# A fixed order of slots for layer 0's dense sums and for layer 1's support stage

## The chip, the cores and the metric

The kernel runs on one core of one Trainium2 chip. The time is the device time of one execution in microseconds (us), the median of several runs. A core has TensorE (PE in the profile, with its weight loads as a row of their own, PEld), VectorE (DVE), ScalarE (ACT), GpSimd (POOL) and SyncE (SP), which here only issues DMAs. Each engine takes its instructions in the order in which they stand in its queue; an instruction that waits holds up all that stand behind it.

## What is computed

A four-layer graph network on 4096 nodes with 256 features and a dense 4096 x 4096 matrix of zeros and ones. Only the first two layers matter here:

```python
# layer 0: attention with 8 heads; entries off the graph have logit 0, not minus infinity
node_feats = (x @ W.T + b).reshape(4096, 8, 32)
logits = leaky_relu(logit_parent[:, None] + logit_child[None, :], 0.2)
logits = where(adj != 0, logits, 0.0)
out = einsum('ijh,jhc->ihc', softmax(logits, axis=1), node_feats)
x = layernorm(x + out)
# layer 1
support = x @ weight
out = (diagonal(adj) + adj) @ support + bias
x = layernorm(x + out)
```

Layer 2 (attention with a top-p cut, two diffusion steps) and layer 3 (mean of neighbours, a product, relu) follow.

## The kernel before, in words

Rows are handled in 32 blocks of 128 (`NB = 32`, `P = 128`). Instructions outside `manual_schedule` regions are put in order for each engine by a scheduler that simulates the program: an instruction may be moved ahead of others that stand before it in the source, as soon as the simulation finds its inputs and its buffers ready. Inside a `manual_schedule` region the named engines keep the order of the source. Buffers are given out from pools: a name with `bufs=2` has two buffers in turn, and the third tile of the name waits until the first is read for the last time. Before the change there are two such regions, both in layer 2.

**Layer 0, dense sums (`sums0`, L412 to L565).** A first part computes the node features and the factors of the softmax. Then comes the loop over pairs of blocks, L530 to L565. It reads the adjacency matrix once, in 128 groups of 512 KB: for each pair `b` eight groups `g` of four block columns. A group is loaded into `a` by two DMAs on SP's queue (L538), cast by VectorE to `ar` (L540), multiplied by ACT into bytes `nb` (L543, twice), stored as bytes to the DRAM tensor `nad` from POOL's queue (L544), and used by TensorE as the stationary operand of 32 matmuls against `src`, the node features in a high and a low part (L550). `a`, `ar` and `nb` have two buffers each. The sums of a pair, `pz`, stay in PSUM (four buffers[...]) until VectorE closes the pair (L559 to L564) and the result `zd` is stored (L565).

In the same loop `factored(b)` prepares what the later attention multiplies: for each block VectorE builds `vf` (L515 to L517), and in three rounds ACT copies it to bfloat16, `gb` (L521, L523, L525), and VectorE subtracts the copy (L522, L524), so that three bfloat16 parts hold one float32. Two DMAs on POOL's queue then store `gb` to the DRAM tensor `gmd` (L527). `vf` and `gb` have two buffers. In the source two blocks are factored ahead of each pair's groups; nothing in their inputs depends on the pair.

`early_mask` (L248 to L260) prepares a part of the first mask of the attention in four of the later pairs: a load of bytes from `nad` (L255) and, before the first part, one of `gmd` (L251), both on SP's queue, and three VectorE instructions in each of these pairs (two L257, one L260).

After the loop the kernel reads a flag (L366) and, since the factors fit, skips the general path. The attention of layer 0 (L328 and around) follows, from 610 to 1322 us. Its accumulator `acc` [...]has two buffers. The layernorms of finished rows run on POOL between heads; those of the last eight blocks, the list `later`, are left to layer 1.

**Layer 1 (`layer1`, L766 to L811).** Its support stage takes four blocks at a time (`g`): TensorE transposes the rows of X (L108), ACT copies the result to one of two tiles `xT` (L109), TensorE multiplies it by `w1` (L781; each is two matmuls in the profile[...]) into `ps_sup`, and `split` takes that to XD in a high part by ACT (L126) and a low part by VectorE (L127). `ps_sup` has two buffers. `attention_weights` (L752 to L764) runs ahead of it and uses `ps_sup` too. The layernorms of `later` stand in groups 1 to 4, all on VectorE but for the two small POOL instructions of each (L88, L89). After the stage a row for the diagonal is made (L786).

The product (L793 to L811) then multiplies the adjacency with XD: four pieces per block are cast back from bytes (L204 on ACT, L206 on VectorE; eight buffers), written to DRAM as float32 for layer 2 by `keep` (L154 to L168, on SP's queue, with the diagonal piece added on POOL, L164), and used in 32 matmuls (L802) per block. The bytes come by DMAs on ACT's queue (L189). The scheduler mixes the first of this work into the support stage.

Of the kernel before, what the change touches and what calls it, by code (L numbers as in the profile page):

```python
# [23 lines left out]
P = 128  # L24
# [31 lines left out]
class Net:  # L56
# [136 lines left out]
    def adj_pieces(self, pool, nas, b, G=8):  # L193

        nc = self.nc
        at = b * P % self.IT
        if at == 0:
            nas[:] = self.bytes_of(pool, b)
        pieces = []
        for g in range(self.NB // G):  # L200
            a = pool.tile([P, G, P], F32R, name="adj_piece", bufs=2 * (self.NB // G))
            edges = nas[g][:, :, at:at + P].bitcast(FP8)
            if g % 2:
                nc.scalar.mul(a, edges, 2.0 ** 5)  # L204
            else:
                nc.vector.tensor_scalar_mul(a, edges, 2.0 ** 5)  # L206
            pieces.append(a)
        return pieces
# [6 lines left out]
    def layer0(self):  # L215
# [7 lines left out]
        with ExitStack() as ctx:  # L223
# [24 lines left out]
            def early_mask(work, part):  # L248

                if part == 0:  # L250
                    nc.sync.dma_start(gm0, gmd[0, :, 0:8, 0])  # L251
                two = slice(2 * part, 2 * part + 2)
                na0, sg0 = (work.tile([P, 2, H, C1], F32, name=name).rearrange("p s h c -> p (s h c)")[:, :512]
                            .bitcast(dt).rearrange("p (k i) -> p k i", k=2) for name, dt in (("nf", U8), ("v", FP8)))
                nc.sync.dma_start(na0, nad[0, :, two, :])  # L255
                for k in range(2):
                    nc.vector.tensor_scalar(sg0[:, k, :], first, nlc[:, 2 * part + k, 0:1], 2.0 ** -5,  # L257
                                            op0=ALU.is_ge, op1=ALU.mult, saturate=False)
                bits = [t.rearrange("p k i -> p (k i)").bitcast(U32) for t in (gt0[:, two, :], sg0, na0)]
                nc.vector.tensor_tensor(*bits, ALU.bitwise_and)  # L260

# [100 lines left out]
            self.later = later  # L362

# [48 lines left out]
    def sums0(self, both, nlc, fac, lpd, nad, zd, gmd, then, early_mask):  # L412
# [6 lines left out]
        with ExitStack() as ctx:  # L419
# [91 lines left out]
            def factored(b):  # L511

                v = work.tile([P, H, 2, C1], F32, name="vf")
                part = lambda i, k: src[:, b, i, k].rearrange("p (h c) -> p h c", h=H).bitcast(F32)
                nc.vector.tensor_add(v[:, :, 1, :], part(0, 0), part(0, 1))  # L515
                nc.vector.tensor_add(v[:, :, 0, :], part(1, 0), part(1, 1))
                nc.vector.tensor_mul(v[:, :, 0, :], v[:, :, 0, :], elc[:, b].unsqueeze(2).to_broadcast([P, H, C1]))  # L517

                gb = work.tile([P, H, 3, 2 * C1], BF16, name="gb")
                v = v.rearrange("p h s c -> p h (s c)")  # L520
                nc.scalar.copy(gb[:, :, 0, :], v)  # L521
                nc.vector.tensor_sub(v, v, gb[:, :, 0, :])  # L522
                nc.scalar.copy(gb[:, :, 1, :], v)  # L523
                nc.vector.tensor_sub(v, v, gb[:, :, 1, :])  # L524
                nc.scalar.copy(gb[:, :, 2, :], v)  # L525
                for half in range(2):
                    nc.gpsimd.dma_start(gmd[half, :, b], gb[:, half * H // 2:(half + 1) * H // 2].rearrange("p h s c -> p h (s c)"))  # L527

            G = 4
            for b in range(0, NB, 2):  # L530
                it, i = divmod(b * P, IT)
                pz = [psz.tile([P, 2, 512], F32, name="pz") for _ in range(2)]
                for q in range(2):
                    factored(b + q)
                for g in range(NB // G):
                    a = work.tile([P, 2, G, P], F32, name="a")
                    for q in range(2):
                        nc.sync.dma_start(a[:, q], self.adjt[b + q, :, g * G:(g + 1) * G, :])  # L538
                    ar = work.tile([P, 2, G, P], F32R, name="ar")
                    nc.vector.tensor_copy(ar, a)  # L540
# [3 lines left out]
                    nc.gpsimd.dma_start(nad[it, :, g * G:(g + 1) * G, i:i + 2 * P], nb.rearrange("p g q i -> p g (q i)"))  # L544
                    for q in range(2):
                        for k in range(G):
                            jc = g * G + k
                            for s in range(2):
                                for t in range(2):
                                    nc.tensor.matmul(pz[q][:, t, :W], ar[:, q, k, :], src[:, jc, t, s],  # L550
                                                     start=(jc == 0 and s == 0), stop=(jc == NB - 1 and s == 1))
                if NB - 12 <= b < NB - 4:
                    early_mask(work, (b - NB + 12) // 2)
                for q in range(2):
                    zt = work.tile([P, 2, H, C1], F32, name="zt")
                    by_head = [t.rearrange("p (h c) -> p h c", h=H) for t in
                               (pz[q][:, 0, :W], pz[q][:, 1, :W], total)]
                    of_row = lambda i: fac[:, i, b + q].unsqueeze(2).to_broadcast([P, H, C1])
                    nc.vector.tensor_mul(zt[:, 0], by_head[0], of_row(2))  # L559
                    nc.vector.tensor_sub(zt[:, 1], by_head[2], by_head[1])  # L560
                    nc.vector.tensor_scalar(self.deg[:, b + q:b + q + 1], zt[:, 1, 0, C:C1], -1.0, float(N),
                                            op0=ALU.mult, op1=ALU.add)
                    nc.vector.tensor_mul(zt[:, 1], zt[:, 1], of_row(3))
                    nc.vector.tensor_add(zt[:, 0], zt[:, 0], zt[:, 1])  # L564
                    (nc.sync if b == NB - 2 else nc.scalar).dma_start(zd[b + q], zt[:, 0])  # L565
# [186 lines left out]
    def attention_weights(self, psum):  # L752
# [3 lines left out]
        for c in range(2):  # L756
            pt = psum.tile([P, 512], F32, name="ps_sup")
            nc.tensor.transpose(pt[:A, :P], aw1[:, c, :], self.ident)
            nc.scalar.copy(w1[:, c, :], pt[:A, :P])
        for c in range(2):  # L760
            pt = psum.tile([P, 512], F32, name="ps_sup")
# [4 lines left out]
    def layer1(self):  # L766
        nc, tc, NB, D, X = self.nc, self.tc, self.NB, self.D, self.X
        with self.ctx1 as ctx:
# [4 lines left out]
            self.attention_weights(psum)  # L773
            for g in range(NB // 4):
                xT = self.transposed(psum, work, X[:, 4 * g:4 * g + 4, :], "xT", out=self.xT1[g % 2])
                if 1 <= g <= 4:
                    self.layernorm(work, self.later[g - 1], self.later[g - 1])
                for q in range(4):
                    ps = psum.tile([P, 512], F32, name="ps_sup")
                    for c in range(2):  # L780
                        nc.tensor.matmul(ps[:, :D], xT[:, c, q * P:(q + 1) * P], w1[:, c, :],  # L781
                                         start=(c == 0), stop=(c == 1))
                    self.split(XD[:, 4 * g + q], ps[:, :D])
            pd = psum.tile([P, 512], F32, name="ps_sup")
# [7 lines left out]
            nas = []  # L792
            ahead = self.adj_pieces(work, nas, 0)  # L793
# [1192 lines left out]
```

## Time and profile before

| what | us |
|---|---|
| runs before, median of 3 (lowest to highest) | 3985.94 (3985.65 to 3993.06) |
| the profiled execution | 3996.39 |
| its span, first to last instruction | 3994.6 |
| setup of layer 0, to the first L550 | 0 to 72.7 |
| dense sums, L550 | 72.7 to 605.1 |
| attention of layer 0, L328 | 610.5 to 1322.1 |
| support stage, to the last L786 | 1322.1 to 1395.65 |
| last L802 of the product | 1623.4 |
| layers 2 and 3 | to 3994.6 |

Times within the run are microseconds from the start of the span. A group of the profile is one line of code on one engine: after `|` come its busy time, the mean nanoseconds of one, and after the next `|` the engine's idle time just before such instructions, with what ended it (`<-`). A row of the window view gives a stretch, its length, the busy time of each engine with the number of instructions in brackets, then the TensorE clock that was granted (1.00 is full), the mean busy share of the 16 DMA engines, and GB/s.

### The profile page before, as it was taken

The numbers are of one execution on the slowest core, as the hardware profiler recorded it, in microseconds if no ns is written. First come the engines' busy times: TensorE is split into PE (matmuls) and PEld (weight loads), VectorE is DVE, ScalarE is ACT, GpSimd is POOL, SyncE is SP. The second block draws the span as 40 slices with busy tenths as digits, with TensorE's granted clock in tenths as the row PEclk, the third lists the DMA queues.
The fourth block names the chain that finished last, engine by engine and source line by source line (L and its number), as shares of the span: only waits on it lengthen the run. The fifth ranks groups of instructions, "written<-read, shape, count | busy, mean of one in ns | idle before, by whom it ended". The sixth has DMA issues, their size and how long they took to land. (4 is left out here: it accounts for less than half of the span.)

```text
span 3994.6 us, 68784 instructions
## 1 busy us (share of the span) xinstructions
PE 3901.5 (98%) x25081; PEld 3375.7 (85%) x25081; DVE 2997.9 (75%) x6645; ACT 2747.6 (69%) x5121; POOL 1160.1 (29%) x1394
## 2 busy tenths in 40 slices
PE   8899998999999899999999999999999999999899
PEld 7899998999999788668888888875888888888687
DVE  7642228999999544567878787847999999999364
ACT  5533227999999422468888888835988888888232
POOL 1321111111344022311111111114556555555311
PEclk9999999999999999999999999999999999999999
DMA  4765557335222498533232323373333333335641
GB/s 127 230 207 174 179 169 220 96 98 145 70 77 71 153 354 331 164 120 102 93 102 93 103 92 103 100 240 107 101 120 100 107 113 111 103 107 183 203 164 48
DMA packets 317563, 557.36 MB, mean 140 GB/s; under 512 B 72806, under 2 KB 139894, under 8 KB 313110
## 3 DMA queue, kind: packets, MB, share of 16 engines
q1 hardware_dynamic: 242528, 396.99, 31.2%
q0 software_dynamic: 32224, 98.75, 7.7%
q10 hardware_dynamic: 42454, 57.04, 4.3%
q8 instruction: 203, 3.33, 0.3%
q14 instruction: 154, 1.26, 0.1%
HBM read 386.71 MB, written 165.94 MB: 138 GB/s over the span
## 5 line engine op out<-in xcount | busy, mean ns | idle before, releaser
L1359 PE MATMUL ps_a<-X,aT 128*128 128x256 f32 x4096 | 968.9, 379 | 1.3 <-ACT h L1503 1.1
L1359 PEld LDWEIGHTS ps_a<-X,aT 128*128 128x128 f32 x4096 | 773.2, 190 | 127.0 <-issue 3.5
L328 PE MATMUL acc<-gm,gt 128*128 128x198 bf16 x8192 | 702.7, 248 | 14.1 <-DMA gm<-gmd 5.6
L328 PEld LDWEIGHTS <-gt 128*128 128x128 fp8e4 x8192 | 700.7, 97 | 16.2 <-issue 11.2
L273 ACT ACTIVATE sg<-lpb,nlc 128x1024 fp8e4<-128x1024 f32 x632 | 664.4, 1138 | 48.4 <-DVE gt L275 33.7
L550 PE MATMUL pz<-src,ar 128*128 128x264 f32 x4096 | 512.8, 288 | 20.1 <-DVE ar L540 18.1
L550 PEld LDWEIGHTS pz<-src,ar 128*128 128x128 f32 x4096 | 509.6, 191 | 23.2 <-DVE ar L540 21.4
L180 PE MATMUL ps_r<-XD,adj_piece 128*128 128x512 f32 x1888 | 528.4, 414 | 0.0
L1086 ACT ACTIVATE ja<-e,nc 128x2048 uint8<-128x2048 f32 x240 | 481.3, 2006 | 2.0
L1352 ACT COPY aT<-ps_tp 128x512 f32<-128x512 f32 x512 | 296.6, 579 | 214.4 <-PE ps_tp L1350 212.0
L180 PEld LDWEIGHTS ps_r<-XD,adj_piece 128*128 128x128 f32 x1888 | 332.9, 189 | 68.8 <-issue 12.9
L1151 DVE MAX8 cand<-v 128x8 f32<-128x256 f32 x1024 | 347.3, 414 | 4.4
L1201 DVE SCALAR_TENSOR_TENSOR e<-e,edge 128x512 f32<-128x512 f32 x512 | 346.6, 749 | 2.1
L543 ACT ACTIVATE nb<-ar 128x512 uint8<-128x512 f32 x256 | 147.8, 624 | 268.2 <-DVE ar L540 268.0
L1350 PE MATMUL ps_tp<-ident,e 128*128 128x128 f32 x2048 | 308.1, 273 | 1.9 <-DVE e L1201 1.9
L1147 DVE SCALAR_TENSOR_TENSOR v<-e,hi 128x2048 f32<-128x2048 f32 x128 | 303.1, 2368 | 2.3
L1350 PEld LDWEIGHTS ps_tp<-ident,e 128*128 128x128 f32 x2048 | 256.8, 142 | 53.6 <-DVE e L1201 3.0
L267 DVE TENSOR_SCALAR sg<-lpb,nlc 128x1024 fp8e4<-128x1024 f32 x384 | 286.1, 781 | 6.6 <-SPq L366 4.4
L995 ACT ACTIVATE e<-ps_logit 128x1024 f32<-128x1024 f32 x256 | 260.2, 1027 | 27.1 <-PE ps_logit L993 26.7
L993 PE MATMUL ps_logit<-kT,q 128*128 128x512 f32 x1024 | 273.5, 409 | 1.8 <-ACT e L995 1.4
L540 DVE CAST ar<-a 128x1024 fp32r<-128x1024 f32 x128 | 89.1, 696 | 247.2 <-PE pz L550 244.3
L802 PE MATMUL ps_adj<-XD,adj_piece 128*128 128x512 f32 x1024 | 244.8, 398 | 1.2 <-POOL ln_var L88 1.2
(401 smaller groups left out, 5614.4 us busy)
## 6 DMA issues: line engine op xcount, KB each, us to landing
adj_piece<-adjs SPq DMA_DIRECT2D x552, 256.0 KB, 2.8
a<-in_adjt_dram SPq DMA_DIRECT2D x256, 256.0 KB, 2.9
adjs<-adj_piece SPq DMA_DIRECT2D x96, 512.0 KB, 3.4
na<-nad SPq DMA_DIRECT2D x64, 512.0 KB, 4.3
lpb<-lpd POOLq DMA_DIRECT2D x32, 512.0 KB, 4.2
nad<-nb POOLq DMA_DIRECT2D x128, 128.0 KB, 2.7
na<-nad ACTq DMA_DIRECT2D x16, 1024.0 KB, 5.7
gmd<-gb POOLq DMA_DIRECT2D x64, 198.0 KB, 3.7
```

Source lines behind the costliest of these rows:

```text
L180: nc.tensor.matmul(ps, a[:, k, :], rhs(jc).rearrange("p s d -> p (s d)"), start=(jc == 0), stop=(jc == self.NB - 1))
L267: nc.vector.tensor_scalar(sg[:, k, :], lpb, nlc[:, 4 * g + k, h:h + 1], 2.0 ** -5, op0=ALU.is_ge, op1=ALU.mult, saturate=False)
L273: nc.scalar.activation(sg[:, k, :], lpb, AF.Sign, scale=-1.0, bias=nlc[:, 4 * g + k, h:h + 1], saturate=False)
L328: nc.tensor.matmul(acc[:, q, :6 * C1], gt[:, k, q * P:(q + 1) * P], gm0[:, jc, :] if head0 else gm[:, jc, hh, :], start=(jc == 0 and q % 2 ...
L550: nc.tensor.matmul(pz[q][:, t, :W], ar[:, q, k, :], src[:, jc, t, s], start=(jc == 0 and s == 0), stop=(jc == NB - 1 and s == 1))
L1086: nc.scalar.activation(ja, e[:, s * HALF:(s + 1) * HALF], f, bias=nc1, accum_out=fs[:, i + s:i + s + 1])
L1147: nc.vector.scalar_tensor_tensor(v, ec, hi, ec, op0=ALU.is_lt, op1=ALU.mult, accum_out=sb[:, s:s + 1])
L1151: nc.vector.max(cand[:, 8 * j:8 * j + 8], v[:, k * 256:(k + 1) * 256])
L1201: nc.vector.scalar_tensor_tensor(ec, ec, edge[:, j:j + 1], ec, op0=ALU.is_ge, op1=ALU.mult)
L1350: nc.tensor.transpose(pt[:, k * P:(k + 1) * P], e[:, jc * P:(jc + 1) * P], self.ident)
L1352: nc.scalar.copy(aT, pt)
L1359: nc.tensor.matmul(pa[:, :D], aT[:, k * P:(k + 1) * P], X[:, jc, :], start=(jc == 0), stop=(jc == NB - 1))
```

## The change

The dense loop of layer 0 becomes one `manual_schedule` region for all five engines. It is written as 128 slots, one per group: in slot `n` the load of slot `n+2` and the cast (with `nb` and the store to `nad`) of slot `n+1` stand ahead, then, in the first two slots of a pair, the closing of one block of the previous pair, then a quarter of `factored` for one block, then in the slots 3 and 5 of four pairs half of `early_mask`, then the slot's own 32 matmuls. `factored` and `early_mask` are cut into steps by `yield`. The closing of the last pair stands behind the loop.

```diff
+            def load(n):
+                if n < slots:
+                    b, g = n // groups * 2, n % groups
+                    loaded[n] = a = work.tile([P, 2, G, P], F32, name="a")
                     for q in range(2):
                         nc.sync.dma_start(a[:, q], self.adjt[b + q, :, g * G:(g + 1) * G, :])
...
+            def cast(n):
+                if n < slots:
...
+                    ready[n] = ar = work.tile([P, 2, G, P], F32R, name="ar")
+                    nc.vector.tensor_copy(ar, loaded.pop(n))
...
+            with tc.manual_schedule(engines={ET.PE, ET.Activation, ET.DVE, ET.Pool, ET.SP}):
+                load(0)
+                load(1)
+                cast(0)
+                before = None
+                for b in range(0, NB, 2):
+                    pz = [psz.tile([P, 2, 512], F32, name="pz") for _ in range(2)]
+                    masks = early_mask(work, (b - NB + 12) // 2) if NB - 12 <= b < NB - 4 else iter(())
+                    for g in range(groups):
+                        n = b // 2 * groups + g
+                        load(n + 2)
+                        cast(n + 1)
+                        if g % 4 == 0:
+                            stages = factored(b + g // 4)
+                        if before and g < 2:
+                            closed(b - 2, g, before[g])
+                        next(stages)
+                        if g in (3, 5):
+                            next(masks, None)
+                        ar = ready.pop(n)
...
```

`factored` yields after the three operations that build `vf`, after the first copy, after the first subtraction with the second copy, and at its end:

```diff
+                v = v.rearrange("p h s c -> p h (s c)")
+                yield
                 gb = work.tile([P, H, 3, 2 * C1], BF16, name="gb")
-                v = v.rearrange("p h s c -> p h (s c)")
                 nc.scalar.copy(gb[:, :, 0, :], v)
+                yield
                 nc.vector.tensor_sub(v, v, gb[:, :, 0, :])
                 nc.scalar.copy(gb[:, :, 1, :], v)
+                yield
                 nc.vector.tensor_sub(v, v, gb[:, :, 1, :])
                 nc.scalar.copy(gb[:, :, 2, :], v)
                 for half in range(2):
 ...
+                yield
```

At the end of layer 0 the transposes of the first four blocks of X for layer 1 are added, into a tile of `acc`:

```diff
+            acc = psum.tile([P, Q, 256], F32, name="acc").rearrange("p q c -> p (q c)")
+            for c in range(2):
+                half = acc[:, c * 512:(c + 1) * 512]
+                for q in range(4):
+                    nc.tensor.transpose(half[:, q * P:(q + 1) * P], X[:, q, c * P:(c + 1) * P], self.ident)
+                nc.scalar.copy(self.xT1[0][:, c, :], half)
```

The support stage of layer 1 becomes a region in a fixed order as well. `ps_sup` has four buffers instead of two; the transposes of the next four blocks stand between the second and third block of each group; the layernorms of `later` stand in groups 0 to 3, their scaling on POOL instead of VectorE; the bytes for the product are asked for after group 1, and the four pieces of its first block are cast after groups 4 to 7. `adj_pieces` is cut so that one piece can be cast by `adj_part`; pieces are otherwise made as before.

```diff
+            with tc.manual_schedule(engines={ET.PE, ET.Activation, ET.DVE, ET.Pool, ET.SP}):
+                setup = self.attention_weights(psum)
+                next(setup)
+                for g in range(NB // 4):
+                    xT = self.xT1[g % 2]
+                    for q in range(4):
+                        ps = psum.tile([P, 512], F32, name="ps_sup", bufs=4)
+                        for c in range(2):
+                            nc.tensor.matmul(ps[:, :D], xT[:, c, q * P:(q + 1) * P], w1[:, c, :],
+                                             start=(c == 0), stop=(c == 1))
+                        self.split(XD[:, 4 * g + q], ps[:, :D])
+                        if q == 1:
+                            if g == 0:
+                                for _ in setup:
+                                    pass
+                            if g < NB // 4 - 1:
+                                self.transposed(psum, work, X[:, 4 * g + 4:4 * g + 8, :], "xT", out=self.xT1[(g + 1) % 2])
+                    if g < 4:
+                        self.layernorm(work, self.later[g], self.later[g], nc.gpsimd)
+                        if g == 1:
+                            nas[:] = self.bytes_of(work, 0)
+                    else:
+                        ahead.append(self.adj_part(work, nas, 0, g - 4))
```

The product's loop, layers 2 and 3 and the number of matmuls are not changed.

## The prediction

> **What bounds the kernel now.** TensorE does, nearly everywhere; so I look for the places where it is not fed. First the page, parts 1 and 2, and the groups of two stretches:
>
> ```profile
> PE 3901.5 (98%) x25081; PEld 3375.7 (85%) x25081; DVE 2997.9 (75%) x6645; ACT 2747.6 (69%) x5121; POOL 1160.1 (29%) x1394
> PEclk9999999999999999999999999999999999999999
> ```
>
> 98% busy leaves 93 us idle in the span. Busy time also counts slow-clocked work, so I count matmuls per time. The window view (matmul records in brackets after PE busy, then granted clock, DMA share) splits the dense sums of layer 0, 72.7 to 605.1 us:
>
> ```profile
> 100.00:240.00 140.00, 120.30 (x907) 117.25 (x907) 97.80 (x203) 78.40 (x136) 53.61 (x83) 0.95 0.72 233
> 240.00:605.00 365.00, 365.00 (x2982) 365.00 (x2980) 102.80 (x207) 106.18 (x184) 69.40 (x93) 1.00 0.54 174
> 120.00:130.00 10.00, 6.98 (x37) 6.76 (x36) 5.54 (x11) 4.99 (x9) 3.40 (x5) 0.67 0.59 190
> ```
>
> After 240 us a matmul takes 365.0/2982 = 0.1224 us without a gap. Before 240 us the same loop is slower. The groups of 80 to 240 us say why (idle before each, and its releaser):
>
> ```profile
> L550 PE MATMUL pz<-src,ar 128*128 128x264 f32 x1070 | 140.8, 294 | 19.7 <-DVE ar L540 18.1 <-DVE deg L561 1.5
> L522 DVE TENSOR_TENSOR vf<-vf,gb 128x528 f32<-128x528 f32 x30 | 21.2, 706 | 28.0 <-ACT gb L521 27.9
> L521 ACT CAST gb<-vf 128x528 bf16<-128x528 f32 x30 | 19.0, 633 | 41.8 <-DMA gmd<-gb 36.3 <-issue 2.3 <-DVE v L257 1.3
> ```
>
> Read from the bottom: ACT's copy into `gb` waits for the store of `gb` two blocks back; VectorE's L522 waits for ACT; the cast of `ar` (L540) stands behind L522 in VectorE's queue; TensorE waits for the cast. All 32 blocks of `factored` are pushed through by 240 us, so their stores crowd each other. Then layer 1, 1322 to 1397 us, groups and waits:
>
> ```profile
> L781 PE MATMUL ps_sup<-w,xT 128*128 128x256 f32 x128 | 34.3, 411 | 8.3 <-DVE XD L127 8.3
> L127 DVE TENSOR_TENSOR XD<-ps_sup,XD 128x256 fp32r<-128x256 f32 x32 | 13.3, 423 | 29.6 <-ACT XD L126 29.6
> ACT adj_piece L204 <- DMA adjs<-adj_piece: 8.8, 2, 5.7
> PE ps_sup L758 <- DVE red L334: 1.9, 1, 1.9
> ```
>
> The same pattern: ACT's casts of later adjacency pieces (L204) wait for stores, with the support's own copies behind them, and with two `ps_sup` buffers TensorE soon stops.
>
> **Layer 0, the slots.** 16 pairs x 8 groups = 128 slots of 32 matmuls, 32 x 0.1224 = 3.92 us each. Work of eight slots (31.3 us):
> - VectorE: 8 casts x 0.70, two blocks of `factored` (3 x 0.43 + 2 x 0.705 each), two `closed` (4 x 0.43 + 0.15 each) = 5.6 + 5.4 + 3.7 = 14.7 us. Worst slot: 0.70 + 1.87 + 1.29 = 3.86 us; the cast goes first in it and is made a slot ahead.
> - ACT: 16 `nb` x 0.624 + 6 `gb` x 0.63 = 13.8 us, and two issues of `zd`, each behind its `closed` and ahead of `gb`; `ar` comes free late only if this passes 3.9 us.
> - POOL: 8 `nad` issues x 0.75 + 4 `gmd` x 0.60 = 8.4 us. The `gmd` issues wait for ACT's last copy, `nad` of the next slot behind them; a `gb` buffer now has 8 slots to be stored, where 36.3 us were waited.
> - SP: the `a` loads run two slots ahead, as far as two buffers allow. The early mask's loads move past them from 193 to 201 us to the pairs that start at blocks 20 to 26; they then read what was stored long before, so SP's waits of 5.4 us for `nad` and 4.2 us for `gmd`, with `a` loads behind them, go. The mask's VectorE work (8 x 0.77 + 4 x 0.69 = 8.9 us in eight slots) lies in slots with 1.4 us at most of other VectorE work; were this cover gone, 8.9 us is what it could cost.
> - TensorE's four `pz` buffers are two pairs' worth, so `closed` of a pair has the eight slots of the next one before a buffer is wanted.
>
> So nothing here sets the pace but TensorE. Floor: 4096 x 0.1224 = 501.4 us. At the start it still comes out of a pause: 51 records in 72.7 to 80 us took 7.3 us for 6.2, so 1.0 more. 532.4 - 502.4 = 30.0 us; I take off 1.0 for leftover waits: **29 us**. The listing of each engine's order shows the same two casts ahead of the setup's end and fewer `factored` and mask operations among them; I count nothing.
>
> [...] The longest wait for a cast is 3.0 us[...]. The row of 120 to 130 us shows 0.67 after such a wait (0.83 in 180 to 190 and 220 to 230). Counting matmuls contains that loss; I take the count.
>
> The last slot's two `gmd` stores are issued about 2.4 us before the stage ends; the first `gm` load came 7 us after it. Covered; uncovered it costs their landing, 3.6 us.
>
> **Layer 1.** Now: last L328 ends at 1322.1, last L786 at 1395.65: 73.5 us, with 48 product matmuls (L802) in between. New, by the uninterrupted rows of before (a group of 8 L781 records to the next instruction 1.74 us, 8 transposes 1.28, L786 7.27 for 32):
> - The first transposes go to a spare `acc` buffer (1.28 us), copied at once (2 x 0.59); the setup still waits for `red`, until 1324.0. Products start near 1324.4, not 1327.1.
> - First group: 1.74 + setup 0.9 + 1.28 + 1.74 gives 1330.0; the copy of the second `xT` waits for `wkq` (VectorE, behind the last four X additions, about 1329.9), so the next begins at 1331.2.
> - Six groups of 3.48 + 1.28 = 28.6, one of 3.48, six product matmuls 1.4, the row 7.27: 40.7, ending at **1371.9**. ACT per group 4 x 0.374 + 2 x 0.59 = 2.7 us, 3.8 with a cast or with na issues; VectorE 1.7 + 1.1: both under 4.76. The copies (1.2) hide beside 1.74 of products; four buffers let the copy and subtraction lag a group.
> - 1395.65 - 1371.9 = 23.8. But 48 - 6 = 42 product matmuls are moved behind the stage at (1623.1 - 1396.8)/970 = 0.233: 9.8 us. Gain **14 us**.
> - `na` is issued after group 1, near 1334; 4 MB at the highest rate seen (425 GB/s) need 9.9 us. First cast near 1350. The pieces cast in the stage are first users of their eight buffers, so no store is waited for.
> - POOL's diagonal pieces (L164, 0.55 us) now stand behind four layernorms, and SP's stores of block 0 behind the first of them. Who waits: the first cast of block 2, for its buffer. TensorE needs that cast 58 product matmuls after the stage, at 1385.4; even with POOL free only at 1362.4 (next paragraph) and the longest store seen, 9.7 us, it is in time.
>
> What speaks against it: the layernorm of the last eight blocks goes from VectorE (0.425 us each) to POOL, before the transposes of groups 6 and 7. POOL's nearest row of L96, 1040 to 1300 us beside a full VectorE, is 2.39 us, with 1.24 and 1.59 for the two small ones: 7.6 per layernorm, four 30.4, from 1332 to 1362.4; the last transposes stand at 1357, a stall of 5.4 us. [...] In this stage POOL's small operations took 0.31 and 0.71, a third of the other row, so the low end is nearer: nothing, 5.4 in the range.
>
> TensorE's and ACT's orders between the stages, and TensorE's from early in the product on, are unchanged.
>
> **Sum.** 29 + 14 = 43 us. The profiled execution, 3994.6 us span in 3996.4 us, falls to 3953.4. It lies 0.26% above the median 3985.94; 43 us less there is **3943 us**.
>
> **Rivals.**
> - Layer 1 pays nothing (12%): POOL stalls 5.4 us and the product waits for stores. Against it: 1400 to 1600 us ran full at DMA shares of 0.75 to 1.03. For it: work that filled gaps is gone. 3986 - 29 = 3957.
> - Layer 0 pays half (9%): the fixed order waits where a block's `closed` and `factored` meet, 1 us in each of 16 pairs, so about 15 us. For it: 3.86 of 3.92 us. Against: the cast is first. 3986 - 15 - 14 = 3957.
> - Slower (3%): an `a` buffer's turn is two slots, 7.83 us: cast 0.70 + two issues 0.84 + landing. Landing over 6.3 us stalls TensorE; a mean over 7.0 (0.34 us per slot x 128 = 43) eats everything, 8.0 gives 3943 + 0.85 x 128 = 4052. Medians are 2.8 after 240 us and 3.7 before, the maximum 6.6, and the stores now spread.
> - The order isn't what it says (1%): 3986. The listing of the order shows it is.
>
> **Chances.** The forecast has 75%. Its own range: layer 0 24 to 31, layer 1 8 to 17, so 3938 to 3954. To hold 8 in 10 I reach over both half-gain rivals: 3934 to 3959. A measurement tells 0.2% (8 us) from no change. Faster are the first three cases but for 0.01 of them that may fall short: 0.95; that and the last case are within, 0.02; slower 0.03.
>
> **What would show it.** Dense stage ending near 575; about 1140 records in 100 to 240 at clock 1.00; no wait of TensorE for `ar`; ACT's `gb` no longer behind its store; last L328 to last row matmul about 50 us; no TensorE wait for POOL there. A TensorE wait for `ar` in every eighth slot, or for POOL near the seventh transposes, would prove me wrong.

## The result and the profile after

The changed kernel takes **3946.57 us** (median of 4 runs, 3944.42 to 3947.67), beside 3989.50 us for the kernel before (3985.65 to 3993.09): a ratio of 0.9895, 95% interval 0.9881 to 0.9909, so 42.9 us or 1.05% faster. In a second comparison on one chip it took 3949.03 us beside 3985.50 (0.9906, 0.9892 to 0.9919), 36.5 us.

The page of the changed kernel, parts 1 and 2:

```profile
PE 3879.5 (98%) x25081; PEld 3361.6 (85%) x25081; DVE 2993.1 (76%) x6637; ACT 2742.9 (70%) x5121; POOL 1167.5 (30%) x1402
PEclk9999999999999999999999999999999999999999
```

These rows say as little as they did before: the share of TensorE is 98% again. The stages say more. Windows of the changed kernel in the dense stage of layer 0 (stretch, its length, busy time and instructions of PE, PEld, DVE, ACT, POOL, then granted clock, DMA share, GB/s):

```profile
100.00:240.00 140.00, 140.00 (x1153) 140.00 (x1152) 63.13 (x131) 56.15 (x99) 36.90 (x54) 1.00 0.64 205
240.00:560.00 320.00, 320.00 (x2633) 320.00 (x2632) 147.78 (x298) 127.50 (x225) 85.69 (x125) 1.00 0.65 209
120.00:130.00 10.00, 10.00 (x84) 10.00 (x83) 3.82 (x7) 3.90 (x8) 2.05 (x3) 1.00 0.60 194
```

The early part now runs as fast as the rest: 1153 matmuls in 140 us where there were 907, at a clock of 1.00 where it was 0.95, and no dip at 120 us. VectorE, ACT, POOL and the DMAs have nearly the same load in the first row as in the second; before, the first stretch carried more than its share. The groups of 80 to 240 us, after the last bar the idle time ahead of each:

```profile
L601 PE MATMUL pz<-src,ar 128*128 128x264 f32 x1317 | 160.4, 284 | 0.0
L532 DVE TENSOR_TENSOR vf<-vf,gb 128x528 f32<-128x528 f32 x11 | 7.7, 701 | 0.0
L530 ACT CAST gb<-vf 128x528 bf16<-128x528 f32 x10 | 6.2, 625 | 5.7 <-DVE zt L573 5.7
```

The three rows of the prediction's chain are empty: ACT does not wait for the store of `gb` (36.3 us before), VectorE does not wait for ACT (27.9), TensorE does not wait for the cast (18.1). What ACT still waits for is the closing L573, with nothing urgent behind it. Layer 1, 1285 to 1331 us, groups and then waits:

```profile
L823 PE MATMUL ps_sup<-w,xT 128*128 128x256 f32 x128 | 29.3, 379 | 0.0
L127 DVE TENSOR_TENSOR XD<-ps_sup,XD 128x256 fp32r<-128x256 f32 x32 | 13.0, 419 | 15.0 <-ACT XD L126 14.8
PE acc L370 <- ACT xT L371: 0.7, 1, 0.7
PE ps_sup L798 <- ACT xT L371: 0.7, 1, 0.7
```

VectorE still waits for ACT's half of each split, but with four `ps_sup` buffers and nothing foreign between the splits this no longer reaches TensorE: of its 128 support matmuls none waits (8.3 us before), and its mean duration falls from 411 to 379 ns.

Where the time went, in the two profiled executions (span 3994.6 and 3946.0 us), by the starts of the first and last matmul of each stage:

| stretch | before | after | gained |
|---|---|---|---|
| to the first dense matmul | 72.7 | 72.0 | 0.7 |
| dense stage | 532.3 | 499.7 | 32.6 |
| from there to the attention | 5.5 | 5.6 | -0.1 |
| attention of layer 0 | 711.4 | 707.5 | 3.9 |
| last head to the product's last matmul | 301.5 | 283.5 | 18.0 |
| layers 2 and 3, to the issue of the last store | 2368.2 | 2368.4 | -0.2 |
| from there to the end of the span | 3.0 | 9.3 | -6.3 |
| sum | 3994.6 | 3946.0 | 48.6 |

The two stages that were changed gave 50.6 us in these traces, 7.6 more than forecast. Two rows that nobody changed moved by 3.9 and -6.3; they are taken up below. The timed runs gained 42.9 and 36.5 us, where 43 was forecast. The table gives more because the profiled execution of the kernel before, 3996.39 us, was 7 to 11 us longer than the medians of its timed runs. Traces of kernels with the same code show where: the attention takes 707.5 us in `l1_only` (711.4 here), and the row of layer 1 takes 294.7 in `l0_only` (301.5 here).

### The profile page after: what moved, and what is told of

It reads as the page before. It is cut to its first block, busy times and chain, and to the rows that moved or that the text cites. A ratio compares the mean times of both kernels' runs of the same rounds, so it can differ in the third digit from the quotient of the medians.

```text
span 3946.0 us, 68781 instructions
## 1 busy us (share of the span) xinstructions
PE 3879.5 (98%) x25081; PEld 3361.6 (85%) x25081; DVE 2993.1 (76%) x6637; ACT 2742.9 (70%) x5121; POOL 1167.5 (30%) x1402
## 3 DMA queue, kind: packets, MB, share of 16 engines
q14 instruction: 156, 1.28, 0.1%
## 5 line engine op out<-in xcount | busy, mean ns | idle before, releaser
L601 PE MATMUL pz<-src,ar 128*128 128x264 f32 x4096 | 500.0, 284 | 0.4 <-DVE big L399 0.4
L601 PEld LDWEIGHTS pz<-src,ar 128*128 128x128 f32 x4096 | 499.8, 188 | 0.5 <-issue 0.5
```

## The experiments

Each run is compared with the kernel before on the same chip. "Dense" is the dense stage, "L1" the time from the last head's last matmul to the product's last matmul, both from the one trace of each kernel (first and last matmul by their starts).

| run | us, median (lowest to highest) | before beside it | ratio (95%) | dense | L1 |
|---|---|---|---|---|---|
| l0_only | 3962.20 (3954.47 to 3964.45) | 3986.33 | 0.9937 (0.9923 to 0.9950) | 500.6 | 294.7 |
| l1_only | 3971.89 (3970.33 to 3974.59) | 3986.33 | 0.9963 (0.9950 to 0.9977) | 531.4 | 283.5 |
| l0_free | 3971.80 (3968.56 to 3975.18) | 3986.33 | 0.9965 (0.9953 to 0.9977) | 527.8 | 283.5 |
| front4 | 3975.24 (3970.01 to 3982.68) | 3986.33 | 0.9975 (0.9966 to 0.9985) | 534.1 | 283.6 |
| paced | 3950.06 (3944.23 to 3953.57) | 3987.89 | 0.9904 (0.9889 to 0.9919) | 507.8 | 283.5 |
| front3 | 3956.19 (3952.99 to 3960.22) | 3987.89 | 0.9922 (0.9909 to 0.9936) | 509.8 | 283.6 |
| l1_two | 3949.82 (3949.04 to 3952.13) | 3987.89 | 0.9906 (0.9891 to 0.9921) | 500.7 | 288.1 |
| l1_sched4 | 3954.16 (3952.29 to 3955.08) | 3987.89 | 0.9915 (0.9902 to 0.9929) | 501.0 | 292.8 |
| front4_fill | 3968.30 (3966.10 to 3970.22) | 3985.50 | 0.9954 (0.9941 to 0.9968) | 528.8 | 283.6 |
| ln_dve | 3946.23 (3943.69 to 3955.61) | 3985.50 | 0.9897 (0.9882 to 0.9912) | 500.8 | 284.4 |
| no_early | 3945.56 (3944.37 to 3946.88) | 3985.50 | 0.9896 (0.9881 to 0.9911) | 500.8 | 283.6 |
| after_again | 3949.03 (3946.04 to 3951.57) | 3985.50 | 0.9906 (0.9892 to 0.9919) | 500.0 | 283.6 |

### The two parts alone

The change's diff, half of it taken back: `l0_only` has the region in `sums0` and the old `layer1`, without the early transposes into `acc`; `l1_only` the other way round.

```diff
 l0_only, in layer1
-            with tc.manual_schedule(engines={ET.PE, ET.Activation, ET.DVE, ET.Pool, ET.SP}):
-                setup = self.attention_weights(psum)
...
+            self.attention_weights(psum)
+            for g in range(NB // 4):
+                xT = self.transposed(psum, work, X[:, 4 * g:4 * g + 4, :], "xT", out=self.xT1[g % 2])
...
 l1_only, in sums0
-            with tc.manual_schedule(engines={ET.PE, ET.Activation, ET.DVE, ET.Pool, ET.SP}):
-                load(0)
...
+            for b in range(0, NB, 2):
+                it, i = divmod(b * P, IT)
...
```

> The new dense loop with the old layer 1. Theory (the two parts pay 29 and 14 by themselves): the dense stage lasts about 500 us, as in the changed kernel, and the time is 29 to 33 us below the kernel before. Rival A (the two parts work together, or layer 1 pays nearly nothing in timed runs): 38 us or more below. Rival B (the old loop is longer in the profiled execution than in the timed ones): 20 us or less below.

> The old dense loop with the new support stage of layer 1. Theory: the stage from the last head's last matmul to the last row matmul lasts about 46 us as in the changed kernel, the product runs at 0.234 us a matmul, and the time is 12 to 18 us below the kernel before. Rival (what is gained in the stage comes back in the product behind it, which waits for stores): 5 us or less below, with TensorE waits at the product's matmuls.

Layer 0 alone gains 24.1 us, layer 1 alone 14.4; together 38.5, beside 42.9 and 36.5 for the whole change. Within the noise they add. Layer 1 came as its theory had it. Layer 0 came 5 us short of its theory's lower end in time, though the dense stage has the expected length; the tail of the span (last section) takes 6.3 us of it back.

### Layer 0: the pace or the order?

Three runs and the pair above make a table of two by two. `l0_free` keeps the new source order but lets the scheduler work, which pulls all 32 blocks of `factored` to the first 34 groups again. `front4` keeps the fixed order but factors a whole block in each of the first 32 slots. `paced` is `l1_only`, so the old loop under the scheduler, with each block's factor made to depend on the end of the pair before.

```diff
 l0_free
-            with tc.manual_schedule(engines={ET.PE, ET.Activation, ET.DVE, ET.Pool, ET.SP}):
+            if True:
 front4 (front3: range(3))
-                        if g % 4 == 0:
-                            stages = factored(b + g // 4)
...
-                        next(stages)
+                        for _ in range(4):
+                            next(stages, None)
 paced, in the old factored(b)
+                if b >= 2:
+                    zero = work.tile([P, 1], F32, name="zero")
+                    at = b // 2 * 2 - 1
+                    nc.vector.tensor_scalar_mul(zero, self.deg[:, at:at + 1], 0.0)
+                    nc.vector.tensor_scalar(elc[:, b], elc[:, b], zero, None, op0=ALU.add)
```

In `front4` and `front3` the stages of all blocks form one chain: `stages = (step for c in range(NB) for step in factored(c))`.

> The changed kernel with the new dense loop written in the same source order, but without the region that fixes it, so that the scheduler pulls all 32 blocks of factored features to the first 34 groups again. Theory (it is the fixing that pays, not the new source order): the dense stage lasts 525 us or more, TensorE waits for the cast again, and the time is 20 to 33 us above the changed kernel. Rival (the loads and casts written ahead and the closing in two slots do most of it): the stage lasts 510 us or less, and the time is within 10 us of the changed kernel. The scheduler's choices behind the loop may differ too, so the stage's length counts more than the time.

> The changed kernel with the fixed order kept, but a whole block factored in each of the first 32 slots, the rate at which the kernel before did it, instead of a quarter. Theory R (the rate is what hurts: two buffers of gb cannot be stored fast enough, ACT waits for the store, VectorE behind it, and the casts behind VectorE): the dense stage is 15 to 32 us longer than in the changed kernel, with waits of ACT's gb for its store of 15 us or more. Theory O (the order is what hurts: casts standing behind a waiting subtraction; with each cast first in its slot a block a slot does no harm): the stage is at most 5 us longer.

> The kernel before with the new layer 1, so the old dense loop under the scheduler, but with each block's factoring tied to the end of the sums two pairs' blocks earlier (two VectorE instructions on a handful of numbers a block, which add zero), so that it cannot be pulled ahead of its pair. To be compared with the run that has only the new layer 1, dense stage 531.4 us. Theory (the pace of the factoring is what hurts, by whichever waits; a quarter block a slot on average frees the loop, fixed order or not): the stage lasts 502 to 515 us, and the time is 17 us or more below that run. Rival (it takes the fixed order, casts first): the stage lasts 520 us or more, with TensorE waits for the cast of 10 us or more.

| dense stage, us | order by the scheduler | fixed order |
|---|---|---|
| about a block a slot, at first | 531.4 (l1_only), 527.8 (l0_free) | 534.1 (front4) |
| about a quarter block a slot | 507.8 (paced) | 500.0 (after_again) |

The pace decides. At the old pace the fixed order is worth nothing; at the new pace the scheduler comes within 8 us of it. In time, `paced` gains 37.8 us where `l1_only` gains 14.4, and its ratio, 0.9904, is that of the whole change (0.9895 and 0.9906). `l0_free` gains 14.5, no more than `l1_only`.

A part of these differences is not a matter of waits. The same window, in which TensorE is full at a clock of 1.00, holds more matmuls in the new loop, first `l1_only`, then `l0_free`:

```profile
300.00:570.00 270.00, 270.00 (x2206) 270.00 (x2206) 75.03 (x149) 78.97 (x138) 51.78 (x69) 1.00 0.53 177
300.00:570.00 270.00, 270.00 (x2222) 270.00 (x2221) 78.86 (x158) 80.21 (x140) 51.91 (x69) 1.00 0.54 177
```

A matmul takes 0.1224 us in the three kernels with the old loop (before, `l1_only`, `paced`: 2206 or 2207) and 0.1215 in the eleven with the loop written as slots, fixed or not (2221 or 2222). Over 4096 matmuls that is 3.6 us: all that `l0_free` has over `l1_only`, nearly half of what the fixed order has over `paced`, and a part of the change's 32.6. Why the new loop's step is shorter, no run here shows.

The early window of `paced` is nearly full without any fixed order in layer 0:

```profile
100.00:240.00 140.00, 138.20 (x1116) 137.99 (x1116) 67.39 (x157) 54.91 (x96) 36.82 (x51) 0.99 0.63 208
```

But `front4` did not lose by the chain I had described. It lost 34.4 us, even a little more than theory R said, and yet R's mechanism is not there. Its waits from 66 to 245 us (total, times, longest):

```profile
DVE vf L532 <- ACT gb L530: 26.1, 31, 1.7
ACT gb L533 <- DVE vf L532: 25.4, 32, 1.4
PE pz L601 <- DVE ar L558: 24.3, 23, 2.3
ACT gb L530 <- DMA gmd<-gb: 3.0, 4, 0.9
```

ACT waits 3.0 us for stores, not 15. VectorE and ACT wait for each other, once for each copy and subtraction. VectorE's own timeline in `front4` (start, duration, then in brackets the idle time before) shows one such round, from cast to cast:

```profile
165.27 0.69 DVE L558 CAST ar<-a 128x1024 fp32r<-128x1024 f32 x1
...
166.68 0.43 DVE L526 TENSOR_TENSOR vf<-vf,elc 128x264 f32<-128x264 f32 x1
167.85 0.71 DVE L532 TENSOR_TENSOR vf<-vf,gb 128x528 f32<-128x528 f32 x1 [0.74 <-ACT gb L530]
169.26 0.71 DVE L535 TENSOR_TENSOR vf<-vf,gb 128x528 f32<-128x528 f32 x1 [0.70 <-ACT gb L533]
169.88 0.69 DVE L558 CAST ar<-a 128x1024 fp32r<-128x1024 f32 x1
```

169.88 - 165.27 = 4.61 us a round, 1.44 of it waiting, against a slot of 3.9 us; a round with a closing in it takes up to 6.4. So both theories fell: neither the stores nor casts placed badly, but a round of VectorE that is longer than the slot. Two runs were made to test that: `front3` with three steps a slot, and `front4_fill`, which does the work of `front4` at the same pace but puts the next cast into VectorE's first wait.

```diff
 front4_fill (cast now yields after the cast and after the store of nb)
-                        cast(n + 1)
-                        for _ in range(4):
-                            next(stages, None)
+                        casts = cast(n + 1)
+                        next(stages, None)
+                        next(stages, None)
+                        next(casts, None)
+                        next(stages, None)
+                        next(casts, None)
+                        next(stages, None)
```

> The changed kernel with three steps of the factoring a slot, a block in four thirds of a slot, where the run with a block in each slot lost 34 us to VectorE's rounds of 4.6 us against slots of 3.92. Theory (VectorE's round in a slot is the limit: casts, and subtractions that wait for ACT's copy in the same slot; three steps take about 2.4 to 3.8 us, and pass a slot only where a closing of 1.8 us is added, in two of eight slots): the dense stage is 3 to 14 us longer than in the changed kernel, and the waits fall in the slots with a closing. Rival (the amount of gb stored in a time is the limit): about three quarters of the 34 us, 22 to 30 us, with ACT waiting for stores.

> The run with a whole block factored in each of the first 32 slots (dense stage 534.1 us), the same work and stores at the same rate, only placed otherwise within the slot: the next slot's cast stands between ACT's first copy and the subtraction that waits for it, and the bytes (nb) between the second subtraction's copy and the third copy. Theory (VectorE's round of 4.6 us a slot, 1.44 of it waits for ACT's copies, is what made that run slow): the cast fills one of the two waits, the round falls to about 3.9 to 4.0 us, and the dense stage lasts 508 to 522 us. Rival (the rate of the stores, or of the work, is what hurts): 528 us or more.

`front3` came as the round of VectorE has it: 10.1 us longer than the changed kernel. TensorE waits for the cast nine times, 4.7 us in all, twice in each pair of blocks (33.7 us): the longer wait, up to 0.85 us, is for the cast behind the first closing, as expected; the shorter, 0.35, is not at a closing. The rest is of the same kind, but hidden: a matmul's record lasts 0.28 us while the next one starts after 0.12, so a pause shows as idle time only beyond the first 0.16 us. By the starts of the matmuls, 9.6 of the 10.1 us lie in 35 stretched steps at the beginnings of slots. `front4_fill` missed its theory: 528.8 us, only 5.3 better. The waits, 66 to 300 us:

```profile
ACT gb L530 <- DMA gmd<-gb: 21.0, 15, 3.5
PE pz L608 <- DVE ar L558: 18.1, 13, 2.9
DVE vf L532 <- ACT gb L530: 16.4, 16, 3.1
```

VectorE's round did fall, from 4.6 to 4.0 us where it has no closing and no wait for a store. With it shortened, the stores of `gb` become the limit: ACT's wait for them rises from 3.0 to 21.0 us, and this is the chain of the kernel before (36.3 us in 15 waits there). So two limits lie close together a little above the slot: VectorE's round, and the turn of the two `gb` buffers. At a block a slot whichever the order leaves last takes the time. What would remain with three `gb` buffers was not tried.

### Layer 1: buffers or order?

```diff
 l1_two, everywhere in the support stage
-                        ps = psum.tile([P, 512], F32, name="ps_sup", bufs=4)
+                        ps = psum.tile([P, 512], F32, name="ps_sup")
 l1_sched4, the same in the old stage of l0_only
-                    ps = psum.tile([P, 512], F32, name="ps_sup")
+                    ps = psum.tile([P, 512], F32, name="ps_sup", bufs=4)
```

> The changed kernel with two buffers for ps_sup again, the fixed order kept. Theory B (the two more buffers carry the gain: ACT's and VectorE's split of a block lasts about as long as TensorE's two matmuls pairs, and the two xT copies of each group delay it by 1.2 us): TensorE waits for VectorE's XD again, 7 us or more, the stage lasts 54 us or more, and the time is 8 us or more above the changed kernel's. Theory O (the order carries it): the stage lasts 50 us or less.

> The run with only the new layer 0, so the old layer 1 under the scheduler, with four ps_sup buffers. Theory B (buffers): most of the 14 us of layer 1 come, the product's last matmul lies 10 us or more nearer to the last head's than in the run with only the new layer 0, and TensorE's waits for XD, 7.1 us there, are 2 us or less. Theory O (order, with the early transposes and the product's pieces behind the support's own copies): 5 us or less come.

With two buffers in the fixed order the stage lasts 50.1 us instead of 46.0, and L1 is 4.6 us longer: the order carries most, and the two buffers are worth 4.6 us within it. In time they do not show: the ratio of `l1_two` is 0.9906, as that of `after_again`. This stands between the theories (54 or more, 50 or less), at O's end; TensorE waits 1.4 us for XD, not 7. With four buffers under the scheduler, TensorE's waits for XD fell from 7.1 to 2.3 us, nearly as B said, and L1 by only 1.9 us, as O said. The windows of the stage say where the rest is, first the kernel before, then `l0_only` (the same old stage in another execution), then `l1_sched4`, then the changed kernel:

```profile
1321.90:1395.70 73.80, 62.36 (x281) 50.45 (x279) 29.42 (x77) 25.86 (x56) 6.27 (x12) 0.91 0.60 207
```

```profile
1289.00:1356.10 67.10, 57.85 (x281) 46.97 (x279) 29.30 (x77) 25.63 (x56) 6.25 (x12) 0.97 0.62 228
```

```profile
1288.00:1348.70 60.70, 54.95 (x262) 45.18 (x260) 28.53 (x76) 25.48 (x55) 5.41 (x11) 0.94 0.63 234
```

```profile
1284.80:1331.00 46.20, 44.85 (x239) 38.80 (x237) 24.84 (x66) 24.25 (x54) 14.80 (x18) 1.00 0.66 262
```

TensorE idles 11.4, 9.3, 5.8 and 1.4 us. The kernel before has 42 product matmuls more in its stage than the changed one, worth 9.8 us at 0.233; at full clock it would be busy 44.85 + 9.8 = 54.6 us, and it was busy 62.36. So 7.7 us went into slow work, at a mean clock of 0.91, and 10.1 into idle time: 17.8 of the 18.0 us. The same sum gives 3.2 and 7.9 us for `l0_only`, 11.1 of its 11.2, and for `l1_sched4` (23 matmuls more) 4.7 us of slow work and 4.4 of idle time, 9.1 of its 9.3 us. So beside `l0_only` the four buffers take away 3.5 us of idle time, and 1.5 us more of slow work take a part of it back. The early transposes into `acc` fill the wait at the stage's start, and every trace with them has a clock of 1.00 there; no run takes them away alone, so how much of the new order's gain is theirs stays open.

In time the comparison is less clear. `l1_sched4` gained 33.7 us and `l0_only` 24.1, on two chips; but the timed runs of `l0_only` spread over 10 us, and its trace is that of the shortest of them, 3954.47. Its trace and its median do not describe the same execution, and what made the others longer is not seen.

Two more edits undo single steps of the new stage:

```diff
 ln_dve
-                        self.layernorm(work, self.later[g], self.later[g], nc.gpsimd)
+                        self.layernorm(work, self.later[g], self.later[g])
 no_early
-                        if g == 1:
-                            nas[:] = self.bytes_of(work, 0)
-                    else:
-                        ahead.append(self.adj_part(work, nas, 0, g - 4))
...
+            ahead = self.adj_pieces(work, nas, 0)
             for b in range(NB):
```

> The changed kernel with the layernorms' scaling in layer 1's support stage on VectorE instead of POOL. Theory (POOL or VectorE, four ps_sup buffers cover it): the stage lasts 45 to 48 us, and the time is within 4 us of the changed kernel's. Rival (on VectorE the scaling waits about 1 us for POOL's two small instructions, with the subtractions for XD behind it): TensorE waits for XD, and the stage lasts 49 us or more.

> The changed kernel without the product's bytes and first four pieces within the support stage: they come behind it, as in the product's other blocks. Theory (the stage was also shortened because the product is ready to run on when it ends): TensorE waits for the first pieces behind the stage, and the product's last matmul comes 5 to 14 us later after the last head than in the changed kernel (283.5 us there). Rival (the loads and casts are early enough anyway): 2 us or less later.

Neither step is worth anything that can be measured. With the layernorms on VectorE the stage lasts 46.1 us (46.0), with 0.4 us of a wait for XD. Without the early pieces in the source my theory of 5 to 14 us was wrong: L1 is 283.6 us, the same. The first product matmul starts at 1298.6 us, in the middle of the stage; the fixed region binds its own instructions, and the scheduler still moved the product's casts in between.

### The whole change again

> The changed kernel itself, beside these three on the same chip. Expected: 0.987 to 0.991 of the kernel before, the dense stage 499 to 501 us, layer 1 from the last head to the product's end 283 to 284 us, and timed runs within 4 us of each other, where those of the kernel before lie 7 to 8 us apart.

As expected in the trace: the dense stage 500.0, L1 283.6; the five timed runs lie 5.5 us apart rather than 4, those of the kernel before beside them 7.7. In all eight traces that have the new stage as the change has it, it lasts 46.0 us; the old one, with the same 281 matmuls, lasted 73.8 and 67.0.

No version beat the changed kernel: `no_early` and `ln_dve` lie 3.5 and 2.8 us under `after_again`, with overlapping intervals, and `paced` and `l1_two` lie 1.0 and 0.8 us above it.

## Why the prediction was right

3943 us was forecast, 3934 to 3959 as the range, and 3946.57 was measured. The mechanism held in both stages. That the gain of 42.9 us is so close to the 43 is luck: the two stages gave 7.6 us more than forecast in the traces, the end of the span took 6.3 back, and beside another set of runs of the kernel before the gain is 36.5.

- **What bounds**: right. TensorE not fed, in two places, and counting matmuls over time found both. The chain from the store of `gb` to the cast was the right reading of the kernel before, and `front4_fill` made it appear again in a fixed order. It was not the only limit at that pace: `front4` showed a second one, VectorE's round with ACT, behind it. The prediction's argument that at a quarter block a slot nothing but TensorE sets the pace holds for both.
- **Layer 0, 29 us**: 32.6 in the trace. Waits and slow clock gave the 29 as forecast; the other 3.6 us are the shorter step, which the floor of 4096 x 0.1224 took as fixed and whose cause is not known. The pause at the start was there (54 matmuls from 72 to 80 us, about 1.4 us lost at a clock of 0.81); the 1.0 for leftover waits was not needed. The worst slot, 3.86 of 3.92 us, was no trouble: no TensorE wait for `ar` in 128 slots.
- **Waits or matmuls**: the waits for the cast and the closing that the profile names in the dense stage before add up to 19.6 us, counting matmuls gave 30. The trace gives 29 without the shorter step, so the count was the right choice. The window of 120 to 130 us went from 0.67 to 1.00, and that of 100 to 240 us from 0.95 to 1.00, which is about 7 us by estimate (0.05 x 140); of the 2.4 us beyond both, 1.6 are pauses too short to show as idle (in the trace of before, 16 steps of 0.13 to 0.29 us from matmul to matmul at a clock of 1.00, where 0.1224 is the mean of the full stretch).
- **Layer 1, 14 us**: 18.0 in the trace beside the kernel before, 11.2 beside `l0_only` with the same old stage, 14.4 in time. The prediction named only waits there; 7.7 of the 17.8 us were slow work, which its count of the stage's length contained. The new stage was put at 49.8 us and lasts 46.2. Two terms were too large: eight transposes and their follow-up take 0.87 us, not 1.28 (seven times), and the 1.2 us for the second `xT` copy did not show, since the last two blocks of the first group lie beside it. The 9.8 us for product matmuls moved behind the stage are there: 237.5 us for the rest of the product, 227.7 before.
- **POOL's layernorm**: the row gave 7.6 us each and a stall; I took none, because POOL's two small operations took less in this stage (0.31 and 0.71 us) than in the row (1.24 and 1.59). That its scaling would too was not shown: in the trace of before VectorE does the scaling here. It takes 0.23 + 0.72 + 2.44, about 3.6 us with gaps. Timeline of POOL:

```profile
1299.30 0.23 POOL L88 TENSOR_SCALAR ln_var<-ln_mv 128x2 f32<-128x2 f32 x1 [0.35 <-DVE ln_mv L86]
1299.62 0.72 POOL L89 TENSOR_TENSOR ln_rstd<-ln_var,power 128x2 f32<-128x2 f32 x1
1300.44 2.44 POOL L96 TENSOR_SCALAR X<-X,ln_mv,ln_rstd 128x256 f32<-128x256 f32 x2
```

  One scaling is 1.27 us on average, three times VectorE's 0.425 and about half of the row's 2.39. There was no stall, and `ln_dve` shows that the placement cost nothing either way.
- **The rivals**: layer 1 pays nothing: no, 14.4 us alone. Layer 0 pays half: in time it paid 24.1 of 29, and the waits that this rival rests on are not in the trace. Slower by `a` landing late: the loads landed in 2.7 to 4.1 us, where by the prediction's estimate 6.3 would have begun to stall.
- **What was not foreseen**: 3.9 us in the attention and -6.3 us at the end of the span. The first is not the change's: `l1_only`, with the old dense loop, has an attention of 707.5 us too, and `ln_dve`, with the new one, 711.1. The difference lies in the attention's first 29.5 us: 227 and 226 matmuls at a clock of 0.81 in the kernel before and in `ln_dve`, 272 and 270 at 0.91 and 0.89 in `l1_only` and the changed kernel. The second takes a fifth of layer 0's gain. In the sum the terms that were set too low made it good.

## What to carry to other kernels

Preparation that a scheduler may pull forward because its inputs are ready will be pulled forward, and it can starve the engine that sets the end; spreading it over the loop that has room for it is worth more than fixing the order, and a dependency that ties it to its iteration does most of it. Before believing one chain of waits, ask what limits the same work when that wait is gone: here a second limit stood close behind, and `front4_fill` met it. Count work per time over a stage rather than adding up waits: of the 32.6 us of the dense stage only 19.6 were waits that the profile names, and of the 17.8 of layer 1's stage 7.7 were slow work. And a stage with waits can differ from one execution to the next, as the old one of layer 1 did (73.8 and 67.0 us), so one trace of it is no firm base for a gain.

## What the runs showed of the hardware that was not expected

**The same wait does not always cost clock.** At the start of the old layer 1, TensorE waits 1.90 us for `red` in each trace. In `l1_sched4` and in the kernel before, the clock then falls to 0.50 for some 7 us; in `l0_only` it stays at 1.00 for the next 10 us, until a longer wait, 3.72 us. The windows after that wait, `l1_sched4` first, then `l0_only`:

```profile
1292.00:1294.00 2.00, 2.00 (x9) 1.66 (x9) 1.91 (x9) 0.85 (x2) 0.00 (x0) 0.50 0.03 8
1294.00:1296.00 2.00, 2.00 (x6) 1.56 (x6) 0.89 (x3) 0.32 (x1) 0.00 (x0) 0.50 0.00 0
```

```profile
1292.00:1294.00 2.00, 1.76 (x12) 1.41 (x12) 1.75 (x9) 1.02 (x2) 0.00 (x0) 1.00 0.00 0
1294.00:1296.00 2.00, 2.00 (x14) 1.77 (x13) 1.71 (x5) 0.78 (x3) 0.00 (x0) 1.00 0.04 8
```

What decides whether the clock falls after such a wait, no run here shows. The old stage of layer 1, with its waits of 2 to 4 us, lasted 73.8 and 67.0 us; the new one, without them, 46.0 us in eight traces.

**A tail that goes with the faster kernels.** From the issue of the last store to the end of the span it is 3.0 us in five traces (before, `l1_only`, `l0_free`, `front4`, `front4_fill`), 7.5 in `paced`, and 9.3 in the other eight traces of kernels with a short dense stage. The last 10 us of DMA traffic of the changed kernel contain, beside that store, one packet of the instruction queue, which the traces with 3.0 us do not have. The row of the instruction queue in that view (packets, MB, share of 16 engines' time):

```profile
q14 instruction: 1, 0.01, 0.3%
```

`front3` has the long tail without such a packet, so this packet is not shown to be the cause. Nor is it known whether the tail follows the length of the dense stage or something else that moves with it; no run here tells these apart.
